# ScalarE and VectorE tied to the order of the source in the attention part of an attention and two-convolution kernel

## The chip, the cores and the metric

The kernel runs on one core of a Trainium2 chip. The metric is the device time of one execution in microseconds. Before the change it is 2038.34 us, the median of two executions (2037.73 and 2038.95). The profiled execution has a span of 2038.9 us, with a granted TensorE clock of 0.994 on average.

## The reference

Two layers work on x, 16 images of 128 channels by 32x32 pixels in float32. The first is attention with four heads of 128 channels over the 1024 pixels; the second is two quantised 3x3 convolutions, each with a batch norm over all images.

```python
qkv = einsum('bchw,oc->bohw', x, w_qkv) + b_qkv
scores = einsum('bnc,bcm->bnm', q, k) * c ** (-0.5)
attn = softmax(scores, axis=-1)
out = einsum('bnm,bmc->bnc', attn, v)
x = einsum('bchw,oc->bohw', out, w_out) + b_out + x

out = act_quant(x)
out = batchnorm(conv3x3(out, weight_quant(w1)), gamma1, beta1)
out = act_quant(out)
out = batchnorm(conv3x3(out, weight_quant(w2)), gamma2, beta2)
x = out + x
```

## The kernel before

`fast_path` does the work; a general path that follows is entered only when the softmax sums are out of bounds. It folds the query and key weights into one matrix (`fold_a`) and the value and output weights into another (`fold_b`). For each head g it projects u (`project_u`, L519) in two halves of 512 queries.

The 64 heads (16 images of four) are worked through one after the other, and each but the last in NK = 4 steps. Step k does two things. `scores(g, k)` makes four score groups of 128x512, each in a bank of the PSUM pool `ps_s`, which has three banks in turn, and ScalarE takes each to an exponential (L551). VectorE then adds and subtracts these (L552, L553, L556) so that seven products of half the width do the work of eight in `attend`; L560 and L562 gather the softmax sums. `attend(g, k - 1)`, one step behind, multiplies with the values, adding into four banks of the pool `ps_a`. Every product is two matmuls of 128x64 by 128x512, and two halves of the array work side by side.

After the last step of a head there is a tail, spread over the next head's steps by `at(step, half, fn, ...)`: `run(step, 0)` calls what is due behind the step's scores, `run(step, 1)` what is due behind its attend. With `end = (g + 1) * NK` it is:

- end: `sum_up` 0 (L625, VectorE); behind attend `evacuate` (four copies L595, ScalarE)
- end + 1: `combine` 0 (L605 to L607 ScalarE, L608 VectorE); behind attend `sum_up` 1 (four copies L644)
- end + 2: `combine` 1 (L612, L613), `sum_up` 2 (L648 to L654 VectorE), `project_u` of the head after the next
- end + 3: `combine` 2 (L615, L617, L618), `sum_up` 3 (three copies L657), `project_u`; behind attend `normalise` (L674, L679)

After an image's last head, end + 4 and end + 5 bring `project_out` (L696), so it stands behind the last normalisation; end + 6 the quantisation (L255 to L257) and `transform_rows` (L800); end + 8 and end + 9 four `rows_product` (L816), end + 10 `rows_output` (L823 to L826) and statistics (L298).

The last head goes in 16 units (`score_unit`, `attend_unit`, `normalise_group`), so that the quantisation and the first convolution of the last image can start early. Then come the batch-norm parameters, the second convolution of all images, its statistics, and the sum with the residual.

What sets the order: instructions of one engine run in the order in which they stand in its queue. The framework's scheduler chooses that order at compile time, by readiness and priority in its own estimate, unless a call names an instruction to stay behind (`tc.issue_after`). For TensorE, `product` does that, each matmul behind the one before, so TensorE already has the source's order. ScalarE and VectorE have the scheduler's.

Of the kernel before, what the change touches and what calls it, by code (L numbers as in the profile page):

```python
# [191 lines left out]
def fast_path(  # L192
# [29 lines left out]

    outer = ExitStack()
# [24 lines left out]
    def quantize(b, src, scale, bias, r0=0, r1=H):  # L248

        cut = slice(r0 * W, r1 * W)  # L250
        t = qtp.tile([P, (r1 - r0) * W], F32, tag="qt", name="qt")
        if b == B - 1 and scale == A_LEVELS and r1 == H:
            nc.vector.tensor_scalar(t, src[:, cut], scale, 0.0, ALU.mult, ALU.max)
        else:
            nc.scalar.activation(t, src[:, cut], AF.Relu, bias=bias, scale=scale)  # L255
        nc.vector.tensor_scalar(t, t, A_LEVELS, MAGIC, ALU.min, ALU.add)
        return nc.vector.tensor_scalar(  # L257
            pads[b % NPAD][:, r0 + 1 : r1 + 1, 1 : W + 1],
            t.rearrange("p (h w) -> p h w", w=W),
            MAGIC,  # L260
            None,
            ALU.subtract,
        )
# [82 lines left out]
    def sums_range(b):  # L346
        flat = sums[:, b * NH : (b + 1) * NH, :].rearrange("p g k -> p (g k)")
        nc.vector.tensor_reduce(ext[:, 0, b : b + 1], flat, AX.X, ALU.min)
        nc.vector.tensor_reduce(ext[:, 1, b : b + 1], flat, AX.X, ALU.max)
# [23 lines left out]
    with ExitStack() as ph:  # L373
# [58 lines left out]
        def sum_values(b):  # L432
            t, s = vs[b]
            nc.vector.tensor_tensor(s[:, S3], t[:, 0:NK, BOTTOM], t[:, 0:NK, TOP], ALU.subtract)
            nc.vector.tensor_tensor(s[:, S2], s[:, S3], t[:, NK:, BOTTOM], ALU.subtract)
            nc.vector.tensor_tensor(
                s[:, S1 : S4 + 1],
                t[:, :, TOP].rearrange("p (a k) c -> p a k c", a=2),
                s[:, S2 : S2 + 1].to_broadcast([P, 2, NK, PH]),
                ALU.add,  # L440
            )
# [34 lines left out]
        def fold_a(h):  # L476
            wq_h, wk_h, bq_h = wqk_sb[:, h, 0:P], wqk_sb[:, h, P : 2 * P], wqk_sb[:, h, 2 * P :]
            if h == 0:

                ps = ps_m.tile([P, P], F32, tag="mm", name=f"ps_a_{h}")  # L480
                bias = ps_a.tile([P, 1], F32, tag="a1", name="ps_a_bias")
            else:
                ps = ps_s.tile([P, P + 1], F32, tag="s", name=f"ps_a_{h}")
                bias = ps[:, P:]
            product(ps[:, 0:P], wq_h, wk_h)
            product(bias, wk_h, bq_h)
            nc.vector.tensor_scalar(at_sb[:, h, :], ps[:, 0:P], qscale, None, ALU.mult)
            nc.vector.tensor_scalar(au_sb[:, h : h + 1], bias, qscale, None, ALU.mult)

        def fold_b():  # L490
            ps = ps_s.tile([P, NH, P], F32, tag="s", name="ps_b")
            for h in range(NH):
                product(ps[:, h, :], wvo_sb[:, h, 0:P], wvo_sb[:, h, P : 2 * P])
            nc.scalar.copy(bt_sb, ps)

        def fold_bo():
            ps = ps_s.tile([P, 1], F32, tag="s", name="ps_bo")
            for h in range(NH):
                product(
                    ps,  # L500
                    wvo_sb[:, h, P : 2 * P],
                    wvo_sb[:, h, 2 * P :],
                    start=(h == 0),
                    stop=(h == NH - 1),
                )
            nc.vector.tensor_tensor(bo2_sb, ps, bo_sb, ALU.add)

        def project_u(g, hf, ps=None):
            b, h = heads[g]
            if hf == 0:  # L510
                us[g] = up.tile([P, N], F32, tag="u", name=f"u_{g}")
            if ps is None:
                ps = ps_m.tile([P, HALF], F32, tag="mm", name=f"psu_{g}_{hf}")
            halves(ps, lambda t: at_sb[:, h, LANES[t]], xt[b][:, ts(hf, HALF)])
            dst = us[g][:, ts(hf, HALF)]
            if g == 0 and hf == 0:
                nc.vector.tensor_scalar(dst, ps, au_sb[:, h : h + 1], None, ALU.add)
            else:
                copied = nc.scalar.activation(dst, ps, AF.Identity, bias=au_sb[:, h : h + 1])  # L519
                if g == 0:  # L520
                    load_rest(copied.ins)
# [6 lines left out]
        def last_values(i):  # L528

            b, h = heads[LAST]  # L530
            if i == 0:
                vs["last"] = lastp.tile([P, NCH, P], F32, name="vlast")
            ps = ps_m.tile([P, NK, P], F32, tag="mm", name=f"psv_{i}")
            for n in range(NK):
                halves(
                    ps[:, n], lambda t: xt[b][:, ts(2 * (i * NK + n) + t, PH)], bt_sb[:, h, :]
                )
            nc.scalar.copy(vs["last"][:, ts(i, NK)], ps)
# [4 lines left out]
        def scores(g, k):  # L543
# [4 lines left out]
            for i, (c, m) in enumerate(((0, 1), (1, 1), (0, 0), (1, 0))):  # L548
                ps = ps_s.tile([P, HALF], F32, tag="s", name=f"pss_{g}_{k}_{i}")
                score(ps, b, g, k + NK * c, ts(m, HALF))  # L550
                exps[:] = [nc.scalar.activation(e[:, 2 * c + 1 - m], ps, AF.Exp).ins]  # L551
            nc.vector.tensor_tensor(e[:, T3], e[:, B12], e[:, B22], ALU.add)  # L552
            nc.vector.tensor_tensor(  # L553
                e[:, T1 : T2 + 1 : T2 - T1], e[:, B12 : B11 + 1], e[:, B11 : T3 + 1 : T3 - B11], ALU.subtract
            )
            nc.vector.tensor_tensor(e[:, T4], e[:, T2], e[:, B21], ALU.add)  # L556
            mine = e[:, T4 : T3 + 1]
            if k == 1:
                sides[g] = esp.tile([P, NHF, HALF], F32, tag="es", name=f"es_{g}")
                nc.vector.tensor_tensor(sides[g], es[g, 0][:, T4 : T3 + 1], mine, ALU.add)  # L560
            elif k > 1:
                added = nc.vector.tensor_tensor(sides[g], sides[g], mine, ALU.add)  # L562
                sums_added[:] = [added.ins]
# [28 lines left out]
        def evacuate(g):  # L592
            evs[g] = [evp.tile([P, HALF], F32, tag=f"s{i}", name=f"ev_{g}_{i}") for i in range(4)]
            for to, ps in zip(evs[g], psa.pop(g)):
                nc.scalar.copy(to, ps)  # L595
# [5 lines left out]
        def combine(g, part):  # L601
            sa, sb, s3, sd = evs[g]
            if part == 0:
                y = avs[g, "y"] = evp.tile([P, HALF], F32, tag="y", name=f"y_{g}")
                nc.scalar.copy(y[TOP], s3[BOTTOM])  # L605
                nc.scalar.copy(y[BOTTOM], sd[TOP])
                nc.scalar.copy(sd[TOP], sd[BOTTOM])  # L607
                nc.vector.tensor_tensor(y, sa, y, ALU.add)  # L608
                return
            y = avs[g, "y"]  # L610
            if part == 1:
                nc.scalar.copy(s3[BOTTOM], y[TOP])  # L612
                nc.vector.tensor_tensor(y, y, s3, ALU.add)  # L613
            elif part == 2:
                nc.scalar.copy(sa[BOTTOM], y[BOTTOM])  # L615
                avs[g] = avp.tile([P, N], F32, tag="av", name=f"av_{g}")
                nc.vector.tensor_tensor(avs[g][:, HALF:], y, sd, ALU.add)  # L617
                nc.vector.tensor_tensor(avs[g][:, 0:HALF], sa, sb, ALU.add)  # L618
                evs.pop(g), avs.pop((g, "y"))

        def quadrant_sums(total):
# [3 lines left out]
            nc.vector.tensor_reduce(  # L625
# [8 lines left out]
        def sum_up(g, part):  # L634
# [5 lines left out]
            elif part == 1:  # L640

                side = smp.tile([Q, P // Q, n], F32, tag="side", name=f"side_{g}")
                for a in range(P // Q):
                    nc.scalar.copy(side[:, a, :], sides[g][ts(a, Q), :])  # L644
                sides[g] = side
            elif part == 2:
                total = smp.tile([Q, n], F32, tag="total", name=f"total_{g}")
                nc.vector.tensor_reduce(  # L648
# [4 lines left out]
                nc.vector.tensor_tensor(first, first, second, ALU.add)  # L653
                nc.vector.reciprocal(rinv[0:Q, :], total)  # L654
            else:
                for a in range(1, P // Q):
                    nc.scalar.copy(rinv[ts(a, Q), :], rinv[0:Q, :])  # L657

        def last_sums(part, cut):
# [7 lines left out]
            nc.vector.reciprocal(rinv, ps)  # L667

        def spread(g, cut):
# [4 lines left out]
            nc.vector.transpose(rb, rinv.unsqueeze(2).to_broadcast([P, rinv.shape[1], Q]))  # L674
            return rb

        def normalise(g):
            rb = spread(g, slice(0, N))
            nc.vector.tensor_tensor(avs[g], avs[g], rb, ALU.mult)  # L679

        def project_out(b, hf):
# [14 lines left out]
            nc.vector.scalar_tensor_tensor(  # L696
# [17 lines left out]
        def score_unit(u):  # L714
# [9 lines left out]
            exps[:] = [nc.scalar.activation(e, ps, AF.Exp).ins]  # L724

        def attend_unit(u):
# [8 lines left out]
            elif u == FIRST_UNIT[i] + 1:  # L735
# [6 lines left out]
                nc.vector.tensor_tensor(totals[i], units[(u - 1) // 4][:, (u - 1) % 4], e, ALU.add)  # L742
            else:
                nc.vector.tensor_tensor(total, total, e, ALU.add)
# [13 lines left out]
            elif u + 1 == FIRST_UNIT[i + 1]:  # L758
# [3 lines left out]
                nc.scalar.copy(avs[LAST, i], psa[LAST, i])  # L762
                sides[LAST, i] = quadrant_sums(total)

        def normalise_group(i):
# [5 lines left out]
            nc.vector.tensor_tensor(rb, avs.pop((LAST, i)), rb, ALU.mult)  # L771
            nc.vector.tensor_tensor(x1[:, cut], x1[:, cut], rb, ALU.add)
# [15 lines left out]
        def transform_weights():  # L788
            with tc.issue_after(sums_added[0]):
                nc.vector.tensor_tensor(middle1[:, 1], taps1[:, 0], taps1[:, 2], ALU.add)  # L790
                nc.vector.tensor_tensor(middle1[:, 0], middle1[:, 1], taps1[:, 1], ALU.add)
                nc.vector.tensor_tensor(middle1[:, 1], middle1[:, 1], taps1[:, 1], ALU.subtract)

        def transform_rows(b):
# [3 lines left out]
            for k in (1, 2, 0, 3):  # L798
                x_, y_, op = FOUR[k]
                nc.vector.tensor_tensor(works[b][:, k], pick(x_), pick(y_), op)  # L800

        def rows_product(b, k):
# [13 lines left out]
            nc.scalar.mul(ms[b, inner][:, k // 2], ps, (1.0, 0.5, 0.5, -1.0)[k])  # L816

        def rows_output(b):
# [4 lines left out]
            nc.vector.tensor_tensor(both[:, 0], inner[:, 0], inner[:, 1], ALU.add)  # L823
            nc.vector.tensor_tensor(both[:, 1], inner[:, 0], inner[:, 1], ALU.subtract)
            y = ys[b].rearrange("p (i r w) -> p r i w", r=2, w=W)
            nc.vector.tensor_tensor(y, others, both, ALU.add)  # L826
# [548 lines left out]
```

## Time and profile before

| part of the span | us | PE busy | VectorE busy | ScalarE busy |
|---|---|---|---|---|
| 0 to 110 | 110.0 | 105.5 | 76.9 | 55.1 |
| 110 to 1906, attention | 1796.0 | 1794.2 | 1379.8 | 1062.3 |
| 1906 to 1953, last head and first convolution's end | 47.0 | 44.7 | 29.3 | 22.0 |
| 1953 to 2039, second convolution and output | 86.0 | 56.0 | 75.5 | 59.3 |

The table is the busy time by stretch. In the profile's lines, a number such as L595 is a line of the kernel; PE is TensorE's matmuls, PEld its weight loads, DVE is VectorE and ACT is ScalarE. `out<-in` names what is written and read: `pss` are scores, `e` exponentials, `psa` the banks that attend fills, `ev` their copies, `psu` and `u` the projected queries, `pso` the output projection, `psw` the first convolution's products. All matmuls that go through `product` have the line of that helper, L404, and are told apart by these names. An end of a matmul is modelled; its start is recorded. In a timeline each line is start, length, engine, line, operation, names, shape and count, with idle time before it in square brackets.

### The profile page before, as it was taken

The numbers are of one execution on the slowest core, as the hardware profiler recorded it, in microseconds if no ns is written. First come the engines' busy times: TensorE is split into PE (matmuls) and PEld (weight loads), VectorE is DVE, ScalarE is ACT, GpSimd is POOL, SyncE is SP. The second block draws the span as 40 slices with busy tenths as digits, with TensorE's granted clock in tenths as the row PEclk, the third lists the DMA queues.
The fourth block names the chain that finished last, engine by engine and source line by source line (L and its number), as shares of the span: only waits on it lengthen the run. The fifth ranks groups of instructions, "written<-read, shape, count | busy, mean of one in ns | idle before, by whom it ended". The sixth has DMA issues, their size and how long they took to land. (4 is left out here: it accounts for less than half of the span.)

```text
span 2038.9 us, 24546 instructions
## 1 busy us (share of the span) xinstructions
PE 2000.3 (98%) x9521; PEld 1032.4 (51%) x9521; DVE 1561.4 (77%) x2087; ACT 1198.6 (59%) x2321; POOL 19.5 (1%) x29
## 2 busy tenths in 40 slices
PE   9999999999999999999999999999999999999994
PEld 3444545545454554545455454555545455554441
DVE  5877877777778777777777777777777777776688
ACT  4565556556555655656665565655666466565565
POOL 0000000000000000000000000000000000000020
PEclk9999999999999999999999999999999999999997
DMA  2000000000000000000000000000000000000064
GB/s 74 13 11 21 1 32 1 11 22 11 22 1 32 1 11 21 11 21 1 32 1 11 21 11 22 11 17 26 11 22 12 31 11 11 31 1 11 11 237 167
DMA packets 15132, 52.11 MB, mean 26 GB/s; under 512 B 1696, under 2 KB 2080, under 8 KB 15008
## 3 DMA queue, kind: packets, MB, share of 16 engines
q1 hardware_dynamic: 9584, 32.31, 4.2%
q10 hardware_dynamic: 5424, 18.16, 2.7%
q8 instruction: 76, 1.25, 0.2%
q14 instruction: 48, 0.39, 0.1%
HBM read 30.55 MB, written 19.92 MB: 25 GB/s over the span
## 5 line engine op out<-in xcount | busy, mean ns | idle before, releaser
L404 PE MATMUL pss<-u,x 128*64 128x512 f32 (+1 forms) x4128 | 1043.0, 592 | 2.8 <-ACT u L519 2.6
L551 ACT ACTIVATE e<-pss 128x512 f32<-128x512 f32 x1008 | 580.2, 596 | 339.7 <-PE pss L404 315.7
L404 PEld LDWEIGHTS pss<-u,x 128*64 128x64 f32 x4128 | 456.7, 137 | 438.8 <-issue 323.8
L404 PE MATMUL psa<-e,xs 128*64 128x512 f32 x2016 | 660.8, 592 | 0.0
L404 PE MATMUL psa<-e,xt 128*64 128x512 f32 x1512 | 540.5, 592 | 0.0
L404 PEld LDWEIGHTS psa<-e,xs 128*64 128x64 f32 x2016 | 249.1, 137 | 196.1 <-issue 173.0
L553 DVE TENSOR_TENSOR e<-e 128x1024 f32<-128x1024 f32 x252 | 308.3, 1223 | 23.3 <-ACT e L551 13.7
L552 DVE TENSOR_TENSOR e<-e 128x512 f32<-128x512 f32 x252 | 171.3, 680 | 199.1 <-ACT e L551 197.1
L404 PEld LDWEIGHTS psa<-e,xt 128*64 128x64 f32 x1512 | 188.8, 137 | 162.0 <-issue 128.8
L556 DVE TENSOR_TENSOR e<-e 128x512 f32<-128x512 f32 x252 | 173.8, 690 | 20.3 <-DVE e L553 0.9
L404 PE MATMUL psu<-x,at_sb 128*64 128x512 f32 x512 | 186.1, 600 | 0.7 <-DMA x<-in_x_dram 0.7
L595 ACT COPY ev<-psa 128x512 f32<-128x512 f32 x252 | 134.8, 591 | 52.6 <-PE psa L404 51.8
L644 ACT COPY side<-part 32x32 f32<-32x32 f32 x252 | 54.5, 216 | 180.9 <-DVE part L625 178.7
L562 DVE TENSOR_TENSOR es<-es,e 128x1024 f32<-128x1024 f32 x126 | 154.3, 1225 | 4.2
L404 PE MATMUL pso<-av,bt_sb 128*64 128x512 f32 x504 | 122.8, 592 | 0.0
L674 DVE STREAM_TRANSPOSE rb<-sums 128x1024 f32<-128x1024 f32 (+1 forms) x66 | 80.1, 1213 | 46.5 <-ACT sums L657 46.4
L519 ACT ACTIVATE u<-psu,au_sb 128x512 f32<-128x512 f32 x127 | 87.3, 687 | 39.4 <-PE psu L404 39.4
L404 PEld LDWEIGHTS psu<-x,at_sb 128*64 128x64 f32 x512 | 63.0, 138 | 52.4 <-issue 50.3
L625 DVE TRANSPOSE_TENSOR_REDUCE part<-es 128x32 f32<-128x1024 f32 (+1 forms) x65 | 79.9, 1229 | 2.2
L404 PEld LDWEIGHTS pso<-av,bt_sb 128*64 128x64 f32 x504 | 51.3, 137 | 56.1 <-issue 38.5
L679 DVE TENSOR_TENSOR av<-av,rb 128x1024 f32<-128x1024 f32 x63 | 76.9, 1220 | 1.1
L560 DVE TENSOR_TENSOR es<-e,e 128x1024 f32<-128x1024 f32 x63 | 76.7, 1218 | 0.0
(160 smaller groups left out, 1150.7 us busy)
## 6 DMA issues: line engine op xcount, KB each, us to landing
x_dram<-acc SPq DMA_DIRECT2D x16, 512.0 KB, 4.2
x<-in_x_dram ACTq DMA_DIRECT2D x15, 512.0 KB, 4.5
xt<-in_xT_dram ACTq DMA_DIRECT2D x15, 512.0 KB, 3.6
res<-x_dram SPq DMA_DIRECT2D x1, 7680.0 KB, 30.3
y_dram<-y SPq DMA_DIRECT2D x6, 512.0 KB, 2.6
back<-y_dram SPq DMA_DIRECT2D x1, 3072.0 KB, 11.5
out_dram<-back SPq DMA_DIRECT2D x6, 512.0 KB, 4.6
out_dram<-y SPq DMA_DIRECT2D x5, 512.0 KB, 4.1
```

Source lines behind the costliest of these rows:

```text
L404: done = nc.tensor.matmul(out_, lhsT=lhsT, rhs=rhs, start=start, stop=stop)
L519: copied = nc.scalar.activation(dst, ps, AF.Identity, bias=au_sb[:, h : h + 1])
L551: exps[:] = [nc.scalar.activation(e[:, 2 * c + 1 - m], ps, AF.Exp).ins]
L552: nc.vector.tensor_tensor(e[:, T3], e[:, B12], e[:, B22], ALU.add)
L553: nc.vector.tensor_tensor(e[:, T1 : T2 + 1 : T2 - T1], e[:, B12 : B11 + 1], e[:, B11 : T3 + 1 : T3 - B11], ALU.subtract)
L556: nc.vector.tensor_tensor(e[:, T4], e[:, T2], e[:, B21], ALU.add)
L560: nc.vector.tensor_tensor(sides[g], es[g, 0][:, T4 : T3 + 1], mine, ALU.add)
L562: added = nc.vector.tensor_tensor(sides[g], sides[g], mine, ALU.add)
L595: nc.scalar.copy(to, ps)
L625: nc.vector.tensor_reduce(part, total.rearrange("p (k c) -> p k c", c=Q), AX.X, ALU.add, apply_transpose=True,)
L674: nc.vector.transpose(rb, rinv.unsqueeze(2).to_broadcast([P, rinv.shape[1], Q]))
L679: nc.vector.tensor_tensor(avs[g], avs[g], rb, ALU.mult)
```

## The change

A small class wraps an engine and remembers the last instruction that was made through it. Each new one is tied behind that, as `product` does for TensorE. The calls of ScalarE and VectorE in the attention part, and those of the first convolution that run among them, go through it. It is meant to make the order in which these engines work the one that is written out by the steps, instead of what the scheduler's estimate gives.

```diff
+    class InOrder:
+        def __init__(self, engine):
+            self.engine, self.last = engine, None
+
+        def __getattr__(self, name):
+            def call(*args, **kwargs):
+                with tc.issue_after(self.last) if self.last else nullcontext():
+                    done = getattr(self.engine, name)(*args, **kwargs)
+                self.last = done.ins
+                return done
+            return call
+
+    act, vec = InOrder(nc.scalar), InOrder(nc.vector)
...
             for to, ps in zip(evs[g], psa.pop(g)):
-                nc.scalar.copy(to, ps)
+                act.copy(to, ps)
...
-                exps[:] = [nc.scalar.activation(e[:, 2 * c + 1 - m], ps, AF.Exp).ins]
+                exps[:] = [act.activation(e[:, 2 * c + 1 - m], ps, AF.Exp).ins]
...
-            nc.vector.tensor_tensor(avs[g], avs[g], rb, ALU.mult)
+            vec.tensor_tensor(avs[g], avs[g], rb, ALU.mult)
...
-            nc.scalar.mul(ms[b, inner][:, k // 2], ps, (1.0, 0.5, 0.5, -1.0)[k])
+            act.mul(ms[b, inner][:, k // 2], ps, (1.0, 0.5, 0.5, -1.0)[k])
```

All other lines of the diff make the same replacement. It covers `quantize`, `sums_range`, `sum_values`, the folds, `project_u`, `last_values`, `scores`, `evacuate`, `combine`, the sums, `spread`, `normalise`, `project_out`, the units and groups of the last head, `transform_weights`, `transform_rows`, `rows_product` and `rows_output`. Left as they were are the statistics and the convolution itself (`conv`, `statistics`, `gather`), the batch-norm constants and parameters, the quantisation of the convolution weights, the table load ahead of the square root, every transfer, and all behind the attention part. No step in which something is called is moved: the output projection stands behind the normalisation in the source of both kernels.

## The prediction

> **What bounds the kernel now.** I read the page's first two parts, then the busy time by stretch for one image in the middle, then the timeline of TensorE and ScalarE around the end of a head, then the list of waits, and last the timeline of VectorE at the end of attention.
>
> ```profile
> PE 2000.3 (98%) x9521; PEld 1032.4 (51%) x9521; DVE 1561.4 (77%) x2087; ACT 1198.6 (59%) x2321; POOL 19.5 (1%) x29
> ...
> PE   9999999999999999999999999999999999999994
> ```
>
> ```profile
> 706.14:826.15 120.01, 120.01 (x571) 63.73 (x569) 92.34 (x119) 71.24 (x142) 0.00 (x0) 1.00 0.04 14
> ```
>
> The second line is one image (four heads, 16 steps) in 120.01 us; its columns are PE, PEld, DVE, ACT, POOL, clock. TensorE is busy throughout at full clock. How much of that is rest? Four records of 128x512 start 0.858 us apart nearly everywhere in the timeline. An image has 256 score, 224 attend, 32 u and 32 output records = 544, so 136 x 0.858 = 116.7, plus 24 bf16 records of the first convolution at 0.445 per four = 2.7: 119.4 us. Only 0.6 us of 120.0 is waiting. Over 15 images that is 9 us. So nothing that ScalarE and VectorE do sooner can bring more than about 9 us here, and the question is whether the order of the source makes TensorE wait.
>
> The place where it can is the first step after a head: ScalarE must empty four banks (L595) and take up the exponentials again.
>
> ```profile
> 705.65 1.45 PE L404 MATMUL psa<-e,xs 128*64 128x512 f32 x5
> 706.79 3.75 PE L404 MATMUL pss<-u,x 128*64 128x512 f32 x16
> ```
>
> ```profile
> 706.14 2.08 ACT L595 COPY ev<-psa 128x512 f32<-128x512 f32 x4 [0.80 <-PE psa L404]
> 708.10 0.61 ACT L551 ACTIVATE e<-pss 128x512 f32<-128x512 f32 x1
> 708.74 0.62 ACT L605 COPY y<-ev 64x512 f32<-64x512 f32 x1
> ```
>
> The last attend record starts at 705.65 + 1.45 - 0.59 = 706.51; call this L. Two of the four copies start before or near it (706.14, 706.62), the third at 707.14 = L + 0.63, the fourth at 707.62. L + 0.63 recurs in nearly every head: it is when the last product can be read. So the order of before puts banks that finish early in front. The first exponential starts at L + 1.59 and ends at L + 2.20.
>
> ```profile
> PEld pss L404 <- ACT e L551: 49.2, 126, 1.0
> ...
> ACT e L551 <- DVE es L560: 19.3, 29, 3.1
> ```
>
> Weight loads wait for exponentials 126 times, but mostly under running matmuls; PE itself has 0.2 us of such waits in its row.
>
> **What the Trainium skill says.** "TensorE: Matmul & The Clock Gate", section "Architectural detail: the array is 16× 32×32, not 1× 128×128": ScalarE and VectorE are strict FIFO. The trace agrees: at 38.57 to 39.47 ScalarE runs four side copies (L644), and u (L519), whose last matmul record started at 37.80, starts only at 39.50; the next score starts at 40.24. "PSUM — Partial Sum Buffer", section "Engine vs sequencer instructions": matmuls start and complete in program order. Here that fits the third copy always waiting for L + 0.63. "ScalarE: Activation LUTs", section "What ACT_TABLE_LOAD costs": 186 ns + 0.833 N without a pointer operand, about 93 ns overlapped: 0.61 and 0.52 us at 512; measured 0.59 to 0.61, and 0.48 to 0.52 between starts.
>
> **The change, part by part.** No operation is added or taken away; each `act` or `vec` call is tied behind the one before. TensorE's order was already that of the source.
>
> *Evacuation after a head (63 times).* For the last step (k = 3) the list `seven` puts bank 1's last product fourth, bank 3's fifth, bank 2's sixth and bank 0's seventh. The loop of L595 copies 0, 1, 2, 3. So the first copy waits for the last product, with three copies and the next exponentials queued behind it. Copies start at L + 0.63, 1.11, 1.59, 2.07, the exponential at L + 2.55, ending at L + 3.15; TensorE goes on about 0.05 later (its gap behind an exponential elsewhere), at L + 3.20. What waits is the fourth score group: the score pool has three banks, so it reuses the bank of the first group. In before it starts at L + 2.62 to 2.86 for its first half and at L + 3.00 for its second. Loss: 0.20 (second half late) to 0.58 (first half late); I take 0.4, about the middle, since the halves run side by side. It happens for heads 2 and 3 of each image, and for the first two heads of all: 33 x 0.4 = 13.2. After head 0 of an image (from the second on) 16 output-projection records, 3.4 us, follow the attend; they hide it: 0.
>
> *Head 1 of an image.* Here a convolution product lies between, and its ScalarE scaling (L816) stands in the source before the evacuation.
>
> ```profile
> 796.70 2.05 ACT L595 COPY ev<-psa 128x512 f32<-128x512 f32 x4 [1.03 <-PE psa L404]
> 798.62 0.63 ACT L816 ACTIVATE m<-psw 128x512 f32<-128x512 f32 x1
> ```
>
> L is 797.03; the last bf16 record starts at L + 0.88, so L816 at about L + 1.29, the copies at 1.77 to 3.22, the exponential at 3.70, done at 4.30, TensorE at 4.35. The fourth group is due at L + 3.56 (second half 3.66). Loss 0.7 to 0.8; 15 x 0.75 = 11.3.
>
> *What goes away.* The 0.6 us per image: side copies (L644) and the sums copies (L657) now come steps later than the exponentials that they delay today, and L615 no longer stands before the first exponential at 767.67. 15 x 0.6 = 9, and about 1 in the first images: -10.
>
> *ScalarE elsewhere.* In the step after evacuation it has exponentials to about L + 5.1, three half-tile copies (L605 to L607, 1.9) and four side copies (0.9): done at L + 7.85, before the next exponential at about L + 8.2. L612 and L615 wait for VectorE's y, which is done a step sooner by the same count. u ends 6.3 us into a step of 7.3. All under TensorE: 0.
>
> *VectorE.* A step costs 0.79 + 1.33 + 0.73 + 1.25 = 4.1 us (rows L552, L553, L556, L562 with their gaps), and a step lasts 6.4 to 7.3. The extra work queues: the last head step has av, rb and the product (1.4 + 1.25 + 1.22) and ends 3.3 us into the next step; behind the quantisation and rows of one image it is up to 5.8 us behind. T4 (L556) of a step is due only after the next scores, 9.9 us after its step's start, and the worst I get is 8.5. Hidden: 0. If I am wrong here, it is rival 2.
>
> *Start.* u at 39.50 no longer stands behind the side copies; score restarts about 1 us sooner: -1.
>
> *End of attention.* VectorE today adds up the last exponentials first:
>
> ```profile
> 1934.21 0.69 DVE L744 TENSOR_TENSOR av<-av,e 128x512 f32<-128x512 f32 x1 [1.03 <-ACT e L724]
> 1934.94 0.71 DVE L625 TRANSPOSE_TENSOR_REDUCE part<-av 128x16 f32<-128x512 f32 x1
> 1936.16 0.75 DVE L696 SCALAR_TENSOR_TENSOR acc<-pso,bo_sb,x 128x512 f32<-128x512 f32 x1 [0.51 <-PE pso L404]
> ```
>
> In the source, L742 comes after the first group's normalisation and L744 twice and L625 after the second's, including its wait for ScalarE's relu. Then L742 delays the second acc by 0.8; the second group's pad ends at 1946.2, L744, L744 and L625 end at 1948.4, and the last group's sums, spread, product, add and three steps (3.3 us) end at 1951.7 instead of 1947.9: +3.8. All behind it waits for the statistics, so none is hidden.
>
> Sum: 13.2 + 11.3 - 10 - 1 + 3.8 = +17.3; 2038.3 + 17.3 = 2055.6, say 2055 us (+0.8%). Ends: evacuation at 0.2 and 0.7 gives 6.6 + 10.5, so 2048; at 0.58 and 0.8 it gives 19.1 + 12, so 2062.
>
> **The rivals.** *1, not slower:* the late fourth group is made up because the halves and weight loads re-pair, and only the removal counts: 2038.3 - 10 - 1 + 3.8 = 2031. For it: TensorE runs two halves side by side, and one is up to 0.4 ahead. Against it: a queue that is never idle has nothing to catch up with. *2, clearly slower:* the delay of 0.96 us of the first exponential (L + 2.55 against L + 1.59) reaches TensorE whole in each of 63 heads, by VectorE's queue or a later bank: 60 - 10 - 1 + 3.8 = +53, 2091. For it: VectorE at 77% with up to 5.8 us of backlog. Against it: a slack of 0.4 to 1.0 at the fourth group, and of over 1 us at T4. *3, the end is hidden:* the steady part as forecast, and the last sums cost nothing: 2051; for it, VectorE idles 0.5 to 1 us between the steps there.
>
> **How the numbers follow.** Forecast 0.60, rival 3 0.12, rival 1 0.13, rival 2 0.15. The forecast's own bounds are 2048 to 2062. To leave out no more than 2 in 10, the range takes in most of rival 1 and part of the way to rival 2: 2033 to 2074. Over 2% is 41 us: faster than 1998 would need four times the waiting that TensorE has, 0.01; slower than 2079 is rival 2 and what I haven't seen, 0.14; within, 0.85.
>
> **What would show it.** In the profile after: the first L595 of a head starts at L + 0.63 with an exponential behind the fourth, and the row of waits has PE scores waiting for exponentials, 0.2 to 0.6 us in heads 2 and 3 and 0.7 to 0.8 in head 1, none in head 0; an image takes 120.0 - 0.6 + 1.55, about 121.0 us; L744 runs after L257 of the second group, and the last L257 of attention comes 3.8 us later against the last score. I am wrong if an image takes 119.4 (rival 1), or if scores or attends wait for VectorE's L556, L560 or L562, or exponentials for ScalarE copies in steps other than the first (rival 2).

## The result, and the profile after

The changed kernel takes 2065.39 us (2064.02 and 2066.75) against 2038.34: a ratio of 1.0133, with a 95% interval of 1.0089 to 1.0176. It is 1.3% slower. The forecast was 2055 with a range of 2033 to 2074, so the time lies inside it, on the slow side of the middle. Lines of the kernel move down by 17, and every call of ScalarE and VectorE that goes through the class now has the class's own line, L232. Matmuls have L421.

From the page of the changed kernel, the busy times:

```profile
PE 2014.1 (98%) x9521; PEld 984.7 (48%) x9521; DVE 1559.2 (76%) x2087; ACT 1218.2 (59%) x2321; POOL 19.2 (1%) x29
```

It looks as before: TensorE is 98% busy. The busy time of one image in the middle, from the last attend record of head 2 to the same one four heads later, says more (the columns are as in the prediction):

```profile
713.93:835.44 121.51, 120.81 (x572) 59.96 (x568) 92.22 (x119) 72.51 (x141) 0.00 (x0) 1.00 0.04 14
```

An image takes 121.51 us instead of 120.01, and it does so in all 14 images that lie whole in the steady part. The work of TensorE is the same 119.4 us as worked out in the prediction. So it now waits 2.1 us per image instead of 0.6. Yet its busy time shows only 121.51 - 120.81 = 0.7 us of idle. The Trainium skill says why, under "Perfetto Trace Analysis", section "Tensor Engine Instruction (MATMUL, LD_WEIGHTS)": the end of a matmul in the profile is estimated from its size and an SBUF delay, not observed. The trace fits that: a record is drawn 0.59 us long, and on each half of the array the next starts 0.43 us after its start. Idle time shows only where neither half has a record, and the records are drawn into the next by 0.16 us, so most of the waiting doesn't show. Here it is measured from starts of records alone: on each half, the time by which two starts lie further apart than 0.429 us (0.22 behind a bf16 record).

The whole of the difference between the two profiled spans, 2038.9 and 2064.9 us, divides like this (L is again the start of a head's last attend record):

| part | before | after | difference |
|---|---|---|---|
| start to L of the third head | 106.45 | 106.39 | -0.06 |
| from there to L of head 62 (15 images) | 1804.92 | 1826.16 | +21.24 |
| from there to the end | 127.52 | 132.32 | +4.80 |

The steady part is 14 times 1.50, and 0.25 in the last of the 15 stretches, which has extra products for the last head. Its cause stands at the end of each head. ScalarE and then TensorE in the timeline, head 2 of an image, where L is 713.93:

```profile
714.56 2.05 ACT L232 COPY ev<-psa 128x512 f32<-128x512 f32 x4 [2.56 <-PE psa L421]
716.47 1.62 ACT L232 ACTIVATE e<-pss 128x512 f32<-128x512 f32 x3
```

```profile
712.64 1.45 PE L421 MATMUL psa<-e,xs 128*64 128x512 f32 x5
713.78 0.59 PE L421 MATMUL pss<-u,x 128*64 128x512 f32 x1
713.93 0.59 PE L421 MATMUL psa<-e,xs 128*64 128x512 f32 x1
714.21 4.04 PE L421 MATMUL pss<-u,x 128*64 128x512 f32 x15
```

Before, two copies started ahead of L + 0.63. Now none does: ScalarE stands still for 2.56 us and runs all four copies from L + 0.63, with the first exponential at L + 2.54, done at L + 3.18. The fourth score group starts on both halves at 717.17 = L + 3.24, 0.05 us after that exponential has freed its bank; the 16 score records last from 713.78 to 718.25, 4.47 instead of 3.75 us. Both halves of the array wait, and not equally. The last records before start at L + 1.99 on the half that is ahead and at L + 2.57 on the other, so that the next were due at L + 2.42 and L + 3.00: they are 0.82 and 0.23 us late. In the list of waits (us in total, times, longest):

```profile
ACT ev L232 <- PE psa L421: 103.6, 46, 2.8
PEld pss L421 <- ACT e L232: 76.2, 126, 1.4
PE pss L421 <- ACT e L232: 8.1, 15, 0.6
...
ACT e L232 <- DVE es L232: 1.9, 1, 1.9
```

ScalarE waits for the last attend product, 46 times, 2.3 us on average. Weight loads of the scores wait as often as before but 76.2 us instead of 49.2. The third line has 15 waits, one per image: those are head 1, where the gap is long enough to show as idle time. The fourth line is the one place where exponentials wait for VectorE's sums, which was 19.3 us in 29 waits before.

Head 1, where the convolution's scaling stands first (L is 683.12):

```profile
684.41 0.60 ACT L232 ACTIVATE m<-psw 128x512 f32<-128x512 f32 x1 [2.75 <-PE psw L421]
684.91 2.05 ACT L232 COPY ev<-psa 128x512 f32<-128x512 f32 x4
686.80 1.64 ACT L232 ACTIVATE e<-pss 128x512 f32<-128x512 f32 x3
```

```profile
687.51 1.08 PE L421 MATMUL pss<-u,x 128*64 128x512 f32 x4 [0.56 <-ACT e L232]
```

The first exponential starts at L + 3.68, and the fourth group at L + 4.39, where its halves were due at L + 3.56 and 3.66. A step later ScalarE has the scaling of a later convolution product and four side copies in front of the exponentials:

```profile
693.38 0.60 ACT L232 ACTIVATE m<-psw 128x512 f32<-128x512 f32 x1 [1.55 <-PE psw L421]
693.99 0.90 ACT L232 COPY side<-part 32x32 f32<-32x32 f32 x4
694.79 1.76 ACT L232 ACTIVATE e<-pss 128x512 f32<-128x512 f32 x3
```

That holds back one half of the array alone, by 0.53 us. By starts of records, and in the mean of the two halves, an image loses 0.83 at the end of head 1 and 0.29 a step later, 0.58 in head 2, 0.34 in head 3, nothing in head 0, and 0.09 in small slips elsewhere: 2.13 us. (The figure of a stall has in it the 0.05 us by which the record behind it is late as well: it follows at 0.48 instead of 0.43 us.) The longer waits of before, 0.59 us on one half behind L615 and twice 0.13 on the other, are gone. The difference is 1.5.

VectorE at the end of attention, in the timeline:

```profile
1962.17 0.43 DVE L232 TENSOR_SCALAR pad<-qt 128x512 bf16<-128x512 f32 x1
1962.51 0.68 DVE L232 TENSOR_TENSOR av<-e 128x512 f32<-128x512 f32 x1
...
1966.98 0.30 DVE L232 TENSOR_SCALAR pad<-qt 128x256 bf16<-128x256 f32 x1
1967.19 1.41 DVE L232 TENSOR_TENSOR av<-av,e 128x512 f32<-128x512 f32 x2
1968.64 0.71 DVE L232 TRANSPOSE_TENSOR_REDUCE part<-av 128x16 f32<-128x512 f32 x1
...
1972.35 0.30 DVE L232 TENSOR_SCALAR pad<-qt 128x256 bf16<-128x256 f32 x1
```

The sums of the last exponentials (`av<-e`, `av<-av,e`, `part<-av`) now stand behind the quantisation of the first and of the second group. The last `pad` ends 18.33 us after the start of the last score record (1954.32), where it was 14.74 before: 3.59 us. The rest of the +4.80 of the table is +1.23 behind the last `pad`, where no instruction was tied; that stretch lasts 91.0 to 92.6 us over all the kernels below, and why was not looked into. From L of head 62 to the last score record nothing changes (21.79 and 21.77).

### The profile page after: what moved, and what is told of

Same layout as the page of the kernel before. It is cut to its first block, busy times and chain, and to the rows that moved or that the text cites. A ratio compares the mean times of both kernels' runs of the same rounds, so it can differ in the third digit from the quotient of the medians.

```text
span 2064.9 us, 24510 instructions
## 1 busy us (share of the span) xinstructions
PE 2014.1 (98%) x9521; PEld 984.7 (48%) x9521; DVE 1559.2 (76%) x2087; ACT 1218.2 (59%) x2321; POOL 19.2 (1%) x29
## 5 line engine op out<-in xcount | busy, mean ns | idle before, releaser
L421 PE MATMUL pss<-u,x 128*64 128x512 f32 (+1 forms) x4128 | 1055.0, 592 | 11.9 <-ACT e L232 8.1
L232 DVE TENSOR_TENSOR e<-e 128x512 f32<-128x512 f32 x756 | 655.9, 868 | 402.0 <-ACT e L232 362.3
L232 ACT ACTIVATE e<-pss 128x512 f32<-128x512 f32 x1024 | 601.5, 604 | 587.2 <-PE pss L421 579.3
L421 PE MATMUL psa<-e,xs 128*64 128x512 f32 x2016 | 674.2, 592 | 0.0
L421 PEld LDWEIGHTS pss<-u,x 128*64 128x64 f32 x4128 | 436.4, 137 | 481.7 <-issue 344.1
L421 PE MATMUL psa<-e,xt 128*64 128x512 f32 x1512 | 551.1, 592 | 0.0
L421 PEld LDWEIGHTS psa<-e,xs 128*64 128x64 f32 x2016 | 243.8, 137 | 180.0 <-issue 159.2
L421 PEld LDWEIGHTS psa<-e,xt 128*64 128x64 f32 x1512 | 184.8, 137 | 204.5 <-issue 172.6
L232 ACT COPY ev<-psa 128x512 f32<-128x512 f32 x252 | 129.3, 602 | 109.2 <-PE psa L421 103.6
L421 PE MATMUL psu<-x,at_sb 128*64 128x512 f32 x512 | 186.5, 600 | 1.0 <-DVE au_sb L232 1.0
L232 DVE TENSOR_TENSOR es<-es,e 128x1024 f32<-128x1024 f32 (+1 forms) x134 | 159.8, 1192 | 4.5
L421 PE MATMUL pso<-av,bt_sb 128*64 128x512 f32 x504 | 116.5, 592 | 0.0
L232 ACT ACTIVATE u<-psu,au_sb 128x512 f32<-128x512 f32 x127 | 87.4, 688 | 14.4 <-PE psu L421 11.3
L421 PEld LDWEIGHTS psu<-x,at_sb 128*64 128x64 f32 x512 | 62.2, 138 | 55.1 <-issue 43.9
L421 PEld LDWEIGHTS pso<-av,bt_sb 128*64 128x64 f32 x504 | 59.2, 137 | 48.1 <-issue 47.5
L232 ACT COPY y<-ev 64x512 f32<-64x512 f32 x126 | 77.9, 618 | 3.1
L232 DVE STREAM_TRANSPOSE rb<-sums 128x1024 f32<-128x1024 f32 (+1 forms) x66 | 79.5, 1205 | 0.1
L232 DVE TRANSPOSE_TENSOR_REDUCE part<-es 128x32 f32<-128x1024 f32 (+1 forms) x65 | 79.4, 1222 | 0.1
L232 ACT COPY ev<-y 64x512 f32<-64x512 f32 x126 | 77.6, 616 | 3.1
L232 DVE TENSOR_TENSOR av<-av,rb 128x1024 f32<-128x1024 f32 x63 | 77.2, 1226 | 2.2
L232 DVE TENSOR_TENSOR es<-e,e 128x1024 f32<-128x1024 f32 x63 | 77.2, 1225 | 2.1
L232 ACT ACTIVATE m<-psw 128x512 f32<-128x512 f32 x60 | 35.8, 597 | 67.0 <-PE psw L421 65.2
## 6 DMA issues: line engine op xcount, KB each, us to landing
back<-y_dram SPq DMA_DIRECT2D x1, 3072.0 KB, 11.3
```

The lines of the kernel that those rows point to most:

```text
L232: done = getattr(self.engine, name)(*args, **kwargs)
L421: done = nc.tensor.matmul(out_, lhsT=lhsT, rhs=rhs, start=start, stop=stop)
```

## The experiments

The theory, A where an expectation gives it a letter: TensorE waits because ScalarE's tied queue holds the four copies in an order that begins with the bank that is finished last, in head 1 with a scaling in front; the end is late because of VectorE's tied queue, and nothing else counts. The rival: VectorE's tied queue makes the steady part slow. Each of the nine kernels does all the work of the reference. "Image" is the period of an image in the middle; "end" is from the start of the last score record to the end of the last `pad`. The kernel before, run beside each group on its chip, took 2038.88 (first four), 2037.80 (next three) and 2038.96 us (last two).

| kernel | us | ratio to before, 95% | image | end |
|---|---|---|---|---|
| before | 2038.34 | | 120.01 | 14.74 |
| after | 2065.39 | 1.0133 (1.0089 to 1.0176) | 121.51 | 18.33 |
| e1, ScalarE alone tied | 2071.07 | 1.0156 (1.0139 to 1.0173) | 122.36 | 14.73 |
| e2, VectorE alone tied | 2065.56 | 1.0130 (1.0113 to 1.0147) | 121.49 | 19.56 |
| e3, copies in order of finish | 2051.40 | 1.0059 (1.0042 to 1.0076) | 120.73 | 18.33 |
| e4, and ahead of the scaling | 2030.43 | 0.9958 (0.9942 to 0.9975) | 119.38 | 18.33 |
| e5, and VectorE free at the end | 2027.37 | 0.9951 (0.9934 to 0.9967) | 119.38 | 14.73 |
| e6, only VectorE free at the end | 2059.99 | 1.0104 (1.0087 to 1.0121) | 121.51 | 14.74 |
| e7, only ahead of the scaling | 2058.84 | 1.0102 (1.0085 to 1.0119) | 120.85 | 18.33 |
| e8, e2 with two copies held back | 2042.73 | 1.0020 (1.0013 to 1.0027) | 119.82 | 19.54 |
| e9, before with the copies tied 0, 1, 2, 3 | 2067.68 | 1.0142 (1.0125 to 1.0159) | 121.70 | 14.74 |

### One engine at a time

```diff
-    act, vec = InOrder(nc.scalar), InOrder(nc.vector)
+    act, vec = InOrder(nc.scalar), nc.vector          # e1
+    act, vec = nc.scalar, InOrder(nc.vector)          # e2
```

> Only ScalarE is tied to the order of the source; VectorE is left to the scheduler as before. Theory A (the loss is ScalarE's evacuation order, 1.5 us per image, plus 3.6 us at VectorE's end): an image takes 121.5 us as with the whole change and the end is as before, so about 2062 us. Rival B (VectorE's tied order makes the steady loss): an image near 120 us, 2039 to 2045 us.

> Only VectorE is tied; ScalarE is left to the scheduler. Theory A: an image takes 119.5 to 120.2 us, the last pad comes 18.3 us after the last score as with the whole change, so about 2042 us. Rival B: an image takes about 121.5 us, 2062 us or more.

e1 shows the same stalls at the ends of the heads as the full change, and the end is back at 14.73, so both halves of the theory hold there. But it is 9 us slower than expected: another 0.85 us per image (122.36 against 121.51), nearly all of it behind the end of head 3, comes from VectorE, whose order the scheduler still chooses. Its timeline, and ScalarE's:

```profile
747.38 0.42 DVE L451 TENSOR_TENSOR xs<-xt 128x256 f32<-128x256 f32 x1 [3.50 <-DMA xt<-in_xT_dram]
...
752.24 1.22 DVE L577 TENSOR_TENSOR es<-e,e 128x1024 f32<-128x1024 f32 x1
```

```profile
753.55 1.57 ACT L232 ACTIVATE e<-pss 128x512 f32<-128x512 f32 x3 [1.77 <-DVE es L577]
```

The scheduler put the values of the next image (L451) so early in VectorE's queue that they wait for their transfer, 15 times and 48.7 us in all. Behind them stand the sums that free an exponential's buffer, and ScalarE waits for that buffer. This is read from the trace; no run tests it.

e2 was the miss: 2042 was expected and it is as slow as the full change. The first exponential starts at L + 1.64, so the wait behind the evacuation is indeed gone. Another has taken its place:

```profile
ACT ev L629 <- DVE y L232: 83.3, 45, 2.4
...
ACT ev L632 <- DVE y L232: 80.2, 33, 2.9
```

```profile
716.93 0.90 ACT L661 COPY side<-part 32x32 f32<-32x32 f32 x4
719.72 0.62 ACT L629 COPY ev<-y 64x512 f32<-64x512 f32 x1 [1.89 <-DVE y L232]
720.36 1.57 ACT L568 ACTIVATE e<-pss 128x512 f32<-128x512 f32 x3
```

The scheduler, in an order that it chose for ScalarE, put the half-tile copies of `combine` (L629 and L632, which are L612 and L615 of before) ahead of the exponentials. They need VectorE's `y`, and VectorE's tied queue delivers it late. TensorE loses about 0.9 us in each of two heads of an image. That such a wait holds up everything behind it is what the strict FIFO would have that the prediction cites from the Trainium skill ("TensorE: Matmul & The Clock Gate", section "Architectural detail: the array is 16× 32×32, not 1× 128×128"); here it is 1.89 us with three exponentials behind. That e2 and the full change cost the same is a coincidence of two different waits.

To test that, e8 lets the two copies stay behind the last exponential of the step (`exps[0]` is the one made most recently):

```diff
-                act.copy(s3[BOTTOM], y[TOP])
+                with tc.issue_after(exps[0]):
+                    act.copy(s3[BOTTOM], y[TOP])
```

and the same for `sa`.

> VectorE alone tied, as in e2, and the two half copies of ScalarE that wait for VectorE's y put behind the last exponential of their own step. Theory: in e2 the first of them (L629) stands ahead of the exponentials and waits up to 2.9 us for y behind VectorE's tied queue; behind the exponentials it delays nothing: an image takes 119.5 to 120.1 us, and with the end 3.6 us late 2036 to 2043 us. Rival: TensorE's waits come from VectorE's own sums, and about 121.5 us an image stays.

2042.73, an image of 119.82: 23 of the 27 us that e2 had lost are back. The four copies and the first exponential after a head start as in e2 (L + 0.68, 1.17 and 1.64), so in e2 the two half copies were the cause. In its trace the 15 images take 2.0 us less than before's, and from L of head 62 to the last `pad` it takes 6.5 us more: what is left above before lies in the end. The tied VectorE queue, with these two copies held back, leaves the steady part 0.44 us per image above its floor; the rival falls.

### The order of the copies

```diff
-            for to, ps in zip(evs[g], psa.pop(g)):
-                act.copy(to, ps)
+            banks = psa.pop(g)
+            for i in (1, 3, 2, 0):
+                act.copy(evs[g][i], banks[i])
```

> The whole change, with the four copies of a head in the order 1, 3, 2, 0 in which their banks are finished. Theory A: the first exponential after heads 2 and 3 starts at L + 1.1 instead of L + 2.54 and TensorE does not wait there; head 1 keeps its wait, since the scaling of the convolution product still stands ahead: an image takes 120.4 us, 2048 us. Rival B: no difference, 2065 us.

2051.40 and an image of 120.73, 0.3 above the expected 120.4. In heads 2 and 3 the first exponential starts at L + 1.49 and TensorE doesn't wait; head 1 keeps its stall, its fourth group still at L + 4.39, with the same 15 waits of 8.1 us in the list. The halves come to it further apart than in the changed kernel, and the one that is ahead loses 1.31 us there.

e4 has in addition the copies ahead of the convolution's scaling in head 1:

```diff
-            at(end, 1, evacuate, g)
+            later.setdefault(2 * end + 1, []).insert(0, (evacuate, (g,)))
```

> The copies in the order 1, 3, 2, 0, and ahead of the second convolution product's scaling in head 1. Theory A: no wait of TensorE for exponentials in any head; an image takes 119.4 to 119.5 us, 15 x 2.1 + 1 less than with the whole change, so about 2033 us, with the end still 3.6 us late. Rival B: 2065 us.

One image of e4, and ScalarE after a head:

```profile
700.29:819.67 119.38, 119.38 (x570) 51.43 (x568) 92.09 (x119) 73.87 (x142) 0.00 (x0) 1.00 0.05 14
```

```profile
699.25 0.58 ACT L232 COPY ev<-psa 128x512 f32<-128x512 f32 x1 [1.12 <-PE psa L421]
700.07 1.56 ACT L232 COPY ev<-psa 128x512 f32<-128x512 f32 x3 [0.23 <-PE psa L421]
701.78 0.60 ACT L232 ACTIVATE e<-pss 128x512 f32<-128x512 f32 x1 [0.15 <-PE pss L421]
```

The first copy starts a microsecond before L (700.29), the exponential at L + 1.49. All 14 images of the steady part take 119.38 us, the 119.4 that TensorE's own work needs, and no wait over 0.03 us is left between starts. Both kernels, before and after, are slower than this one: 2030.43.

e7 has that second edit alone, the copies still in the order 0, 1, 2, 3:

> The whole change, with the four copies in the order 0 to 3 but ahead of the second scaling in head 1. Theory: in head 1 the copies run from L + 0.63, the scaling at L + 2.55, the first exponential from L + 3.03 to 3.65, TensorE at 3.7 against 3.56 or a little earlier: 0.15 to 0.45 left of 1.02, so an image takes 120.6 to 121.0 us, 2053 to 2057 us. Heads 2 and 3 keep 0.71 and 0.39.

An image of 120.85 is as expected, 2058.84 us is 1.8 above the expected range. Head 1's fourth group starts at L + 3.73, 0.17 and 0.06 late on the two halves; the stall a step later stays at 0.53, and heads 2 and 3 lose what they lose in the changed kernel.

From the other side, e9 is the kernel before with nothing but the four copies of a head tied to each other in the order 0, 1, 2, 3:

```diff
+            last = None
             for to, ps in zip(evs[g], psa.pop(g)):
-                nc.scalar.copy(to, ps)
+                with tc.issue_after(last) if last else nullcontext():
+                    last = nc.scalar.copy(to, ps).ins
```

> The kernel before, with nothing tied but the four copies of a head to each other in the order 0, 1, 2, 3. Theory: the first copy starts at L + 0.63 and TensorE waits for the exponential behind them, 0.4 and 0.7 us in heads 2 and 3 and about 0.2 in head 1 (the scheduler puts the scaling between the copies): an image takes 121.1 to 121.5 us, 2055 to 2061 us. Rival: the loss needs the tied order of the other instructions too: 120.0 us an image, 2038 us.

It makes the kernel slower by 1.4%, more than expected. ScalarE after a head, L being 770.21:

```profile
770.83 2.05 ACT L597 COPY ev<-psa 128x512 f32<-128x512 f32 x4 [1.81 <-PE psa L404]
```

In heads 2 and 3 the copies and exponentials have the same times against L as in the full change, and TensorE loses 0.50 and 0.72 us there in the mean of its halves. The rest of the excess comes again from half-tile copies, which the scheduler now put ahead of the exponentials:

```profile
720.73 0.62 ACT L614 COPY ev<-y 64x512 f32<-64x512 f32 x1 [0.57 <-DVE y L610]
722.47 0.61 ACT L617 COPY ev<-y 64x512 f32<-64x512 f32 x1 [1.12 <-DVE y L615]
723.11 1.58 ACT L551 ACTIVATE e<-pss 128x512 f32<-128x512 f32 x3
```

These, in head 2, hold one half of the array back by 0.90 us; in head 1 L617, with a scaling behind it, holds one back by 0.33. So the order of the copies does what the theory says without any other part of the change, but in this kernel it couldn't be tried quite alone: a tie on a few instructions moves others.

### The end

```diff
-                with tc.issue_after(self.last) if self.last else nullcontext():
+                with tc.issue_after(self.last) if self.last and not self.free else nullcontext():
...
         for u in range(n_units):
+            vec.free = u >= 12
```

> The whole change, VectorE untied from unit 12 of the last head on. Theory: 3.6 us less than the whole change, 2061.8 us, with 121.5 us per image unchanged. Rival: no difference, 2065 us.

> As e4 (copies 1, 3, 2, 0, ahead of the scaling), and from unit 12 of the last head on VectorE is no longer tied. Theory: the three last sums again come before the second group's normalisation; last score to last pad 14.7 us instead of 18.3, so 3.6 us less than e4: 2026.8 us. Rival: the tail is hidden behind other work, and 2030 us stays.

In e6 (the changed kernel with this alone) the image stays at 121.51 and the end falls to 14.74: 3.59 us, the whole of the lateness. The profiled spans differ by 5.1; another 1.8 is the start, since e6's first attend record stands at 16.97 us and that of the kernel after at 18.74. The time of this record varies from 15.8 to 18.7 us over these kernels, and also between kernels whose source is the same up to there (18.20 in e4, 15.89 in e5); that was not looked into. e5 is e4 with the same edit. VectorE at its end:

```profile
1918.52 1.45 DVE L232 TENSOR_TENSOR av<-av,e 128x512 f32<-128x512 f32 x2
1920.00 0.71 DVE L232 TRANSPOSE_TENSOR_REDUCE part<-av 128x16 f32<-128x512 f32 x1
1920.83 0.75 DVE L232 SCALAR_TENSOR_TENSOR acc<-pso,bo_sb,x 128x512 f32<-128x512 f32 x1
...
1932.26 0.30 DVE L232 TENSOR_SCALAR pad<-qt 128x256 bf16<-128x256 f32 x1
```

The sums stand first again, and the last `pad` ends 14.73 us after the last score record's start. With 2027.37 us it is the fastest of all: 0.5% below before, from an image at its floor and an end as before. That e2 and e8 end 1.2 us later still than the full change was not followed up.

## Why the prediction was right, and where it fell short

- *What bounds the kernel, and the floor.* Right. e4 and e5 run at 119.38 us per image, the sum worked out as 119.4; the gain that was to be had was about 9 us, and 15 times (120.01 - 119.38) is 9.5.
- *Evacuation, the starts.* Right to 0.04: L + 0.63, 1.11, 1.59, 2.06 for the copies, 2.54 and 3.18 for the exponential, 3.24 for TensorE. e3 and e9 show that the order of the banks is the cause.
- *Evacuation, the loss.* Forecast 0.4 per head, between 0.20 for the second half and 0.58 for the first. Measured, in the mean of the halves and with the record behind, 0.58 in head 2 and 0.34 in head 3: 0.92 instead of 0.8 for the two. That it is so near is luck: two errors go against each other. What failed is the step "in before it starts at L + 2.62 to 2.86 for its first half", taken as the due time after the change too. In the changed kernel the first half is due at L + 2.42 in head 2 and at L + 2.90 in head 3, and so loses 0.82, above the bound, and 0.34; the second half is due at L + 3.00 in both, as forecast, and loses 0.23. e3, in the position of head 2 but without the wait, does start its fourth group at L + 2.42, and e8, in that of head 3, at L + 2.90. Where the difference comes from is said in the last section.
- *Head 1.* Starts right to 0.05 (TensorE at L + 4.39 against 4.35), and the loss too: 0.84 and 0.72 on the two halves, 0.78 in the mean, with 0.05 for the record behind, instead of 0.75. The stall a step later was missed, 0.53 us on one half: in "ScalarE elsewhere: 0" the side copies are reckoned only where `combine` comes ahead of them, and the scaling of the later product isn't counted. e7 leaves this stall in place; in e4 it is gone with the first.
- *What goes away.* Right for the three longer waits of an image; slips of about 0.05 us on one half remain, 0.09 per image in the mean.
- *VectorE.* Right for the changed kernel: the exponentials' waits for its sums fell from 19.3 to 1.9 us, and in the list no wait of TensorE's matmuls for it is left between the start and the end. In e2 it is late enough to matter, but only since ScalarE there asks for `y` earlier than the source does.
- *Start.* Forecast -1; L of the first head comes at 45.67 instead of 46.73 us, with the first attend record at 18.74 in both: -1.06, right. The next two L give it back: +0.99, where 0.8 was reckoned less the "about 1 in the first images", so that -0.06 is left at the third head.
- *End.* Forecast +3.8, measured 3.59 in the trace, and e6 takes away 3.59. Rival 3 falls. The 1.23 behind the last `pad` was not foreseen.
- *Sum.* Split as in the table of spans, the prediction had 12.0 + 11.3 - 9 = 14.3 for the 15 images, -1.2 for the start and 4.2 for the end (with head 62): 17.3. The trace has 21.2, -0.06 and 4.8: 26.0. So the larger part of the miss is in the images: TensorE was to wait 1.55 us in each and waits 2.13. Of these 0.58 the stall that was missed is 0.29, heads 2 and 3 are 0.12, head 1 is 0.08, and the slips are 0.09.
- *Rival 1,* the lateness made up, is wrong: the losses between starts add up to the 2.13 us by which an image is above its floor. *Rival 2* is wrong in its cause, and in the changed kernel the 0.96 us didn't reach TensorE whole in a head without a convolution product (0.87 on one half at most, with the record behind).

Three signs that the prediction named need a note. An image was to take 121.0 and takes 121.5. The row of TensorE's own waits for exponentials was to show heads 1, 2 and 3, but shows head 1 only (8.1 us of a loss of 32), because the modelled ends cover the others. And exponentials that stand behind ScalarE copies in a later step, named as a sign of rival 2, are there in head 1, for 0.53 us on one half.

## What to carry to other kernels

A queue that runs in order wants its readers in the order in which their inputs are finished: with banks that end in the order 1, 3, 2, 0, copying 0 first put three copies and the next exponentials behind the last product, and putting them right, ahead of the scaling too, turned +1.3% into -0.4%. When you tie an engine to the source, the source's order becomes part of the tuning, so go through every instruction in it that waits for another engine, and through the end of the kernel as well. Tying one engine and leaving its partner free is not half the change: each alone cost as much as both, by waits that neither order has by itself (tested for VectorE by e8, only read from the trace for ScalarE).

## What was not expected of the hardware

After a stall the two halves of the array start together: the two records of a stalled pair start 7 ns apart (717.168 and 717.175 us in the head 2 shown), whichever half was ahead before. What comes next sets them apart again. In head 1 the late scaling then holds one half back by 0.53 + 0.05 us, and head 2 is reached with the halves 0.58 apart: its last attend record starts at L on one half, and the first score record at L - 0.15 on the other. (The last attend product itself begins at L - 0.43, with the first of its two records: the products start in the order of the source, as the prediction cites, but single records of two products don't.) Head 3 is reached after two slips of about 0.05, with the halves 0.10 apart. This distance sets when the half that is ahead is due: L + 2.42 in head 2, L + 2.90 in head 3. It is why the same exponential, at the same L + 2.54, makes that half 0.82 us late in one head and 0.34 in the next, and the other half 0.23 in both. A due time read from the trace of the kernel before (L + 2.62 to 2.86) is thus not the due time of the changed kernel.
